# A pre-norm decoder layer on one core: two more block transfers of each duo on GpSimd's queue, other durations in the list, one feed-forward for the last two tiles, and the first rows loaded together

## Chip, core and metric

The kernel runs on one core of a Trainium2 chip. The metric is the device time of one execution in microseconds (us). The kernel before was run three times: 1815.37 us median (1815.3 to 1822.67). The profile is of one further execution.

Engines: TensorE (PE; PEld is its weight load), VectorE (DVE), ScalarE (ACT), GpSimd (POOL), SyncE (SP, which here only issues DMAs; SPq is its queue). DMAs are issued by SP, ACT or POOL, and their bytes are moved by 16 DMA engines.

## What is computed

The input `x` has 4 batches of 1024 rows of 256 numbers in float32. Three sublayers follow one another, each on a normalized copy of `x`:

```
x = x + self_attention(layernorm(x))      # 16 heads of 64, 4 key/value heads
x = x + cross_attention(layernorm(x))     # 16 heads of 16, 64 context rows
x = x + feed_forward(layernorm(x))
```

Self-attention is a full softmax over 1024 keys, with no mask. Cross-attention has a mask over the context rows. The feed-forward routes each row: scores against 8 cluster signatures pass through a calibration curve (a sigmoid and a table of 8 knots), the best cluster is taken, the same is done for the 8 entries of that cluster, and the chosen one of 64 table rows gives a small spline and a direction. The direction, scaled by the spline's value, is added to the normalized row, and the sum is normalized again.

## The kernel before, in words

**Tiles.** A tile is 128 rows of `x`; there are 8 per batch (NT), 32 in all. For one tile there are eight chunks of two heads (QC), and a *duo* (`duo`, from L608) handles two chunks, four heads: 128 duos in all.

**A duo.** TensorE computes scores (L631) for two chunks into PSUM; VectorE takes the largest of each row of 1024 (L645); ScalarE takes the exponential (L651) into `prob`; VectorE transposes `prob` in 32x32 blocks (L660). Sixteen DMAs of 128 KB each (L683 to L695, recorded at L689) then carry the blocks to their places in `probT`, so that together a full transpose results. TensorE multiplies `probT` by the values (L712, `av`), and ScalarE copies the result to `heads` (L727). `prob` and `probT` take slots of one pool of five buffers of 16 KB per partition, tag `prob`.

Of a duo's sixteen block transfers, fourteen are issued by SyncE and two by GpSimd (those with `k == 3` and odd `qb`). All sixteen wait for the four transposes of their duo.

**After four duos (`project`).** The softmax denominators are inverted, go to DRAM and come back spread over partitions (`rsD`, `rb`, on SyncE's queue, L758 and L748); GpSimd multiplies `heads` by them (L751); TensorE applies the output weights (L769, `po`); GpSimd adds the result to `x` (L775).

**Cross-attention** runs for two tiles at a time, its wide steps on GpSimd (L900, L909, L923, L924, L931). In the last tile alone (`last`) they are on VectorE.

**Feed-forward** runs for four tiles at a time (TF). The fifth and sixth tile of the last batch have one of two tiles, and the last two tiles have one each. Each has normalizations (`layernorm`: two statistics instructions on VectorE at L444 and L445, four small steps on GpSimd at L449 to L452, one on ScalarE at L457), a transpose (L471, L475), routing (L1153, L1164), two calibrations and selections (L1005 to L1067, L1183, L1184), an indirect DMA from GpSimd per tile that gathers the chosen rows of the table (L1201), the spline (L1221 to L1236), a second normalization, three last steps (L1253) on GpSimd, and the store (L1263). For the very last tile (`last`), the three last steps are on VectorE, the store on SyncE, and the buffers are cuts of the freed `xT` buffer. The tile before it takes the ordinary ones, with its normalized rows in the `kT1` buffer.

**The order of the work** is made before the kernel runs, by a list scheduler (`Flow`). Each task is added with an engine, a planned duration, a key, what it reads and writes, and a lag between its end and the start of who reads it. At each step the scheduler takes the task that could start earliest by the planned durations; ties go to urgent tasks, then to the smaller key. A task marked `hurry` goes ahead of another that would only be done after the urgent one could start. So the planned durations execute nothing, but they set the order of instructions on every engine, and each engine and DMA queue then works in that order.

A buffer is taken by the first task that names it. Every other task that uses the same buffer then needs that first task's end, and its lag, where it is over 1, also on the same engine:

```python
            elif b.first is not t:
                t.need.add(b.first)
...
                o.ready = max(o.ready, t.end + (t.lag if o.engine != t.engine or t.lag > 1 else 0.0))
```

**The first rows.** `normed` loads a batch's rows in four DMAs of two tiles each (L518). For the first batch the four are cuts of one buffer of tag `prob`, with keys -80 to -77 and lags of 3.5 to 6.5. The weights and masks that SyncE loads have keys -40 to -31.

Of the kernel before, what the change touches and what calls it, by code (L numbers as in the profile page):

```python
# [9 lines left out]
F32 = mybir.dt.float32  # L10
# [6 lines left out]
P = 128  # L17
B, S, D = 4, 1024, 256
NT = S // P
TX, TF = 2, 4  # L20
DC = D // P
H, KV, HD = 16, 4, 64
QC = H * HD // P
# [4 lines left out]
NTILES, NCL, TPC, GRID, COMP, NK = 64, 8, 8, 16, 64, 8  # L28
# [182 lines left out]
def decoder(  # L211
# [221 lines left out]
    def layernorm(key, name, src, dst, w, reads, writes):  # L433

        st = Buf("ln", lambda k: (
            small.tile([P, w, 6], F32, tag=f"bnst_{k}", name=f"{name}_st", bufs=1),
            small.tile([P, w, 2], F32, tag=f"bnmv_{k}", name=f"{name}_mv", bufs=1),
            small.tile([P, w], F32, tag=f"bnrs_{k}", name=f"{name}_rs", bufs=1),
        ))

        def stats():
            bn, mv, _ = st.t
            for t in range(w):
                nc.vector.bn_stats(bn[:, t, :], src(t))  # L444
                nc.vector.bn_aggr(mv[:, t, :], bn[:, t, :])  # L445

        def rsqrt():
            _, mv, rs = st.t
            nc.gpsimd.tensor_scalar(rs, mv[:, :, 1], EPS, None, ALU.add)  # L449
            nc.gpsimd.tensor_tensor(rs, rs, minus_half.to_broadcast([P, w]), ALU.pow)  # L450
            nc.gpsimd.tensor_tensor(mv[:, :, 1], mv[:, :, 0], rs, ALU.mult)
            nc.gpsimd.tensor_scalar(mv[:, :, 1], mv[:, :, 1], -1.0, None, ALU.mult)  # L452

        def apply():
            _, mv, rs = st.t
            for t in range(w):
                nc.scalar.activation(dst(t), src(t), AF.Identity, bias=mv[:, t, 1:2], scale=rs[:, t : t + 1])  # L457

        add("DVE", 0.58 * w, key, stats, reads, [st], holds=writes)
        add("POOL", 1.3, key, rsqrt, [st], [st])  # L460
        add("ACT", 0.57 * w, key, apply, [st, *reads], writes)

    def transposed(key, name, src, dst, k, reads, write, w=2):
# [41 lines left out]
    def normed(b, key):  # L505

        xTs[b] = buf("xT", big, DC, S, name=f"ln1_{b}_T")
        parts = x[b].rearrange("(g t p) d -> g p t d", p=P, t=2)

        whole = None if b else Buf("prob", lambda k: work.tile([P, 4 * S], F32, tag=f"prob_{k}", name="ln1_first", bufs=1))  # L510
        for g in range(NT // 2):
            if b:
                n = buf("xn1", big, 2, D, name=f"ln1_{b}_{g}_n")
            else:
                n = Cut(whole, lambda t, g=g: t[:, 2 * D * g : 2 * D * (g + 1)].rearrange("p (t d) -> p t d", t=2))
            at = key(g)
            add(
                "SP", 0.5, at - 2 if b else -80 + g, lambda n=n, g=g: nc.sync.dma_start(out=n.t, in_=parts[g]), writes=[n],  # L518
                lag=3.5 if b else 3.5 + g,
            )  # L520
            get = lambda t, n=n: n.t[:, t, :]
            layernorm(at, f"ln1_{b}_{g}", get, get, 2, [n], [n])
            transposed(at, f"ln1_{b}_{g}", get, lambda: xTs[b].t, g, [n], xTs[b].part(g))
# [81 lines left out]
    def duo(b, d):  # L605
# [73 lines left out]
        if not by_array(b, d):  # L679


            for k in range(4):
                for qb in range(4):  # L683
                    r = (qb + k) % 4

                    engine, queue, cost = ("POOL", nc.gpsimd, 1.0) if k == 3 and qb % 2 else ("SP", nc.sync, 0.64)

                    def carry(qb=qb, r=r, queue=queue):
                        queue.dma_start(  # L689
                            out=probT.t[32 * r : 32 * r + 32, S * qb : S * (qb + 1)],  # L690
                            in_=prob.t[32 * qb : 32 * qb + 32, S * r : S * (r + 1)],
                        )

                    add(
                        engine, cost, at, carry, [prob.part((z, i)) for z in range(2) for i in range(2)],  # L695
                        [probT.part((z, g)) for z in range(2) for g in range(2)], lag=2.3,
                    )
# [291 lines left out]
            add("POOL", 0.73, now + 4, residual, [r, xp], [xp])  # L989


    def calibrated(at, name, score, w, reads, scratch=None):

        n = w * NCL

        def new(k, tag, *shape):
            return small.tile([P, *shape], F32, tag=f"{tag}_{k}", name=f"{name}_{tag}", bufs=1)

        c = scratch or Buf("cal", lambda k: (
            new(k, "cf", n), new(k, "chot", NK - 1, n), new(k, "clow", n), new(k, "cpick", NK - 1, n), new(k, "cval0", n), new(k, "cval1", n),  # L1000
        ))
        no3 = step_no.unsqueeze(2)
# [67 lines left out]
        add("DVE", 0.4, at, second, [m], [m])  # L1070
        return m

    def feed_forward(b, t0, w, at, last=False, before=False):
        name = f"{b}_{t0}"
        n = w * P
        xp = [x_part(b, t0 + t) for t in range(w)]
# [4 lines left out]
        def cut(*shape):  # L1081

            k = 1
            for i in shape:
                k *= i
            a = taken[0]
            taken[0] = a + k
            dims = " ".join(f"d{i}" for i in range(len(shape)))
            sizes = {f"d{i}": shape[i] for i in range(1, len(shape))}
            return lambda t: t.rearrange("p c s -> p (c s)")[:, a : a + k].rearrange(f"p ({dims}) -> p {dims}", **sizes)  # L1090

        def one(f):
            return Cut(whole, f)

        def several(*f):
            return Cut(whole, lambda t: tuple(g(t) for g in f))

        xf = one(cut(w, D)) if last else flat_buf(*(("kT1", big, S) if before else ("xf", big, TF * D)), f"ln3_{name}_n", w, D)
        xT = one(cut(DC, n)) if last else flat_buf("fp", big, TF * GT, f"ln3_{name}_T", DC, n)
        for t in range(w):  # L1100
            layernorm(
# [13 lines left out]
        some = cut(n)  # L1115
        hT = one(lambda t: some(t)[:COMP]) if last else flat_buf("xhalf", work, 512, f"hT_{name}", n, rows=COMP)
        ph, pc = psum1(f"pch_{name}"), psum1(f"pcomp_{name}")
        comp = one(cut(w, 2)) if last else Buf("comp", lambda k: small.tile([P, w, 2], F32, tag=f"comp_{k}", name=f"comp_{name}", bufs=1))

        def compress():  # L1120
            for dc in range(DC):
# [22 lines left out]
        flow.hurry = last  # L1144


        sc = one(cut(w, NS)) if last else Buf("sc", lambda k: small.tile([P, w, NS], F32, tag=f"sc_{k}", name=f"sc_{name}", bufs=1))
        pr = psum1(f"pr_{name}")

        def route():  # L1150
# [12 lines left out]
            "DVE", 0.46, at + 2,  # L1163
            lambda: nc.vector.tensor_copy(sc.t.rearrange("p t n -> p (t n)"), pr.t[:, : w * NS]), [pr], [sc],  # L1164
        )
        m = w * NCL
        cal = several(cut(m), cut(NK - 1, m), cut(m), cut(NK - 1, m), cut(m), cut(m)) if last else None
        c, gates = calibrated(at + 4, f"cc_{name}", lambda: sc.t[:, :, :NCL], w, [sc], cal)
        ch = first_max(at + 5, f"cm_{name}", gates, w, [c])
        wide = [P, w, NCL, TPC]  # L1170
        index = Buf("index", lambda k: small.tile([P, w], mybir.dt.int32, tag=f"tile_{k}", name=f"tile_{name}", bufs=1))
        hot = several(cut(w, NCL, TPC), cut(w, TPC), cut(w)) if last else Buf("hot", lambda k: (
            small.tile(wide, F32, tag=f"hot_{k}", name=f"hot_{name}", bufs=1),
            small.tile([P, w, TPC], F32, tag=f"sel_{k}", name=f"sel_{name}", bufs=1),
            small.tile([P, w], F32, tag=f"tno_{k}", name=f"tno_{name}", bufs=1),
# [14 lines left out]
            nc.vector.tensor_scalar(idx, no, float(NCL * TPC + NCL), None, ALU.add)  # L1190

        add("DVE", 0.4 + 0.15 * w, at + 6, select, [sc, ch], [hot])
        c, gates = calibrated(at + 7, f"cl_{name}", lambda: hot.t[1], w, [hot], cal)
        lh = first_max(at + 8, f"lm_{name}", gates, w, [c])
        add("DVE", 0.45, at + 9, chosen, [lh, ch, hot], [hot, index])

# [2 lines left out]
        for t in range(w):  # L1199
# [8 lines left out]
            add("POOL", 1.05, at + 11, gather, [index], [par.part(t)], lag=3.0)  # L1208


        hh = several(cut(w, GRID), cut(w, GRID), cut(w)) if last else Buf("hh", lambda k: (
            small.tile([P, w, GRID], F32, tag=f"hh_{k}", name=f"hh_{name}", bufs=1),
            small.tile([P, w, GRID], F32, tag=f"h2_{k}", name=f"h2_{name}", bufs=1),
            small.tile([P, w], F32, tag=f"mag_{k}", name=f"mag_{name}", bufs=1),
# [54 lines left out]
    for b in range(B):  # L1269
        at = float(b * steps_of)  # L1270
        normed(b, lambda g: at - 18 + 2 * g if b else -50 + g)
        for w in range(NT // 2):
            if w == 0:
                keys(b, 0, at - 5)
            for c in range(0, QC, 2):
                queries(b, w, c, at + 2 * QC * w + c - 5)
            if w == 0:
                keys(b, 1, at - 1)
                for g in range(NT // 2):
                    value_rows(b, g, at + g / 2)  # L1280
                for g in range(NT // TF):
                    load_x(b, g, at + 2 + 4 * g * QC)
                context(b, at + 10)
            for d in range(QC * w, QC * w + QC):
                duo(b, d)
                if d % (QC // 2) == QC // 2 - 1:
                    project(b, d // (QC // 2))
            t = 2 * w + 1
            if b == B - 1 and w == NT // 2 - 1:

                for k in (t - 1, t):
                    flow.hurry = k == t
                    cross_attention(b, k, 1, at + QC * (k + 1) + 3, k == t)
                    feed_forward(b, k, 1, at + QC * (k + 1) + 6, k == t, k != t)
                continue
            cross_attention(b, t - TX + 1, TX, at + QC * (t + 1) + 3)
            last = TX if (b, t // TF) == (B - 1, NT // TF - 1) else TF
            if t % last == last - 1:
                feed_forward(b, t - last + 1, last, at + QC * (t + 1) + (10 if last == TF else 7))
# [93 lines left out]
```

## Time and profile before

| | |
|---|---|
| profiled execution, its own time | 1819.6 us |
| its span, first to last instruction | 1817.7 us |
| mean granted TensorE clock | 0.943 |
| GpSimd: block transfers, issues x mean | 256 x 533 ns = 136 us |
| GpSimd: idle before its block transfers | 256.8 us |
| TensorE busy, 150 to 250 us | 96.5% |
| TensorE busy, 400 to 410 us | 85.5% |
| TensorE busy, 1700 to 1710 us | 0% |
| DMA bytes, mean rate over the span | 310.18 MB, 171 GB/s |
| first scores (L631) | 34.99 us |
| last TensorE instruction for attention (L769) ends | about 1733 us |

How to read the views: times count from the first instruction. A line of the timeline has start, length, engine and line of the program, what is written from what, and in brackets how long the engine was idle before it and what ended that. The chain of waits follows the work that ended last backwards to what released each step. A busy TensorE is not TensorE at its peak, since matmuls are pipelined. The share of the DMA engines in a stretch is worked out from packet times and can come a little above 1.

### The profile page before, as it was taken

How to read it: one execution, taken by the hardware profiler on the slowest of the kernel's cores; microseconds unless marked ns; L12 is line 12 of the kernel's file. 1: busy time of each engine (PE TensorE's matmuls, PEld its weight loads, DVE VectorE, ACT ScalarE, POOL GpSimd, SP SyncE). 2: the span in 40 equal slices, each digit the busy share in tenths (PEclk: the TensorE clock that was granted, in tenths of full speed). 3: DMA queues.
4: the chain of work that ended last, by engine and by line, in shares of the span. 5: the costliest groups of instructions: out<-in, count | busy, mean ns of one | idle time of the engine just before them, and what ended most of it. 6: DMA issues, size and time to landing. Idle time of an engine off the chain costs nothing.

```text
span 1817.7 us, 28586 instructions
## 1 busy us (share of the span) xinstructions
PE 1597.9 (88%) x9168; PEld 905.3 (50%) x9168; DVE 1523.4 (84%) x2094; ACT 964.6 (53%) x1793; POOL 756.1 (42%) x1156
## 2 busy tenths in 40 slices
PE   6899999998999789998999889998999979998551
PEld 4354555554555445554555445554555534554331
DVE  4889998889878989888888899889896988889365
ACT  3455565656455456655465456565464544564231
POOL 1112435337251554437243464428333264343643
PEclk9899999999999999999999999999999988999665
DMA  4779888757786588866877578876877478785500
GB/s 143 172 181 222 192 205 211 198 140 179 186 198 151 119 209 211 192 170 168 199 185 171 140 180 204 194 188 171 205 186 173 105 183 201 188 203 151 125 8 19
DMA packets 120148, 310.18 MB, mean 171 GB/s; under 512 B 36576, under 2 KB 47712, under 8 KB 120000
## 3 DMA queue, kind: packets, MB, share of 16 engines
q1 hardware_dynamic: 103936, 263.09, 59.8%
q0 software_dynamic: 14960, 42.90, 9.1%
q10 hardware_dynamic: 1104, 2.37, 0.3%
q8 instruction: 74, 1.21, 0.3%
q14 instruction: 74, 0.61, 0.1%
HBM read 35.32 MB, written 4.46 MB: 22 GB/s over the span
## 4 chain that ended last, share of the span: by engine, by line
PE 47%; DVE 18%; SPq 9%; DMA 8%; POOL 7%; ACT 5%; issue 5%; DVEq 0%; POOLq 0%; ACTq 0%
PE s L631 16%; PE av L712 16%; SPq L689 8%; DVE nmax L645 7%; DMA probT<-prob 5%; DVE prob L660 5%; PE po L769 4%; ACT prob L651 3%; PE pq L584 3%; POOL ln_n L1253 2%; DMA rb<-rsD 1%; PE pxp L978 1%; PE pv L556 1%; PE pk L533 1%; PE pxt L944 1%
## 5 line engine op out<-in xcount | busy, mean ns | idle before, releaser
L651 ACT ACTIVATE prob<-s,nmax 128x1024 f32<-128x1024 f32 x512 | 569.9, 1115 | 356.9 <-DVE nmax L645 318.9
L645 DVE TENSOR_REDUCE nmax<-s 128x1 f32<-128x1024 f32 x512 | 598.5, 1209 | 127.4 <-PE s L631 124.6
L660 DVE STREAM_TRANSPOSE prob<-prob 128x1024 f32<-128x1024 f32 x512 | 612.8, 1223 | 42.1 <-ACT prob L651 19.1
L631 PE MATMUL s<-kT,qT 64*128 64x512 f32 x2048 | 566.3, 628 | 31.2 <-ACT prob L651 25.2
L712 PE MATMUL av<-probT,vn 128*64 128x256 f32 x4096 | 507.8, 398 | 45.1 <-DMA probT<-prob 16.9
L712 PEld LDWEIGHTS av<-probT,vn 128*64 128x64 f32 x4096 | 293.3, 142 | 275.2 <-issue 99.1
L631 PEld LDWEIGHTS s<-kT,qT 64*128 64x128 f32 x2048 | 204.9, 189 | 258.4 <-issue 175.0
L689 POOL DMA_DIRECT2D probT<-prob x256 | 136.0, 533 | 256.8 <-DMA probT<-prob 96.2
L751 POOL TENSOR_TENSOR heads<-heads,rb 128x256 f32<-128x256 f32 x128 | 91.8, 735 | 158.4 <-ACT heads L727 93.4
L769 PE MATMUL po<-wo,heads 128*128 128x256 f32 x512 | 128.5, 395 | 16.9 <-POOL heads L751 13.8
L584 PE MATMUL pq<-ln_T,wq 128*128 128x256 f32 x512 | 127.5, 396 | 9.4 <-ACT heads L727 4.0
L900 POOL TENSOR_TENSOR xsc<-xsc,mneg 128x1024 f32<-128x1024 f32 x31 | 73.7, 2379 | 122.9 <-ACT xsc L892 122.7
L769 PEld LDWEIGHTS po<-wo,heads 128*128 128x128 f32 x512 | 94.0, 193 | 55.8 <-POOL heads L751 28.1
L584 PEld LDWEIGHTS pq<-ln_T,wq 128*128 128x128 f32 x512 | 96.1, 194 | 42.1 <-issue 14.5
L651 ACT ACTIVATION_READ_ACCUMULATOR prob<-s,nmax 128x1 f32 x512 | 100.5, 196 | 0.0
L727 ACT COPY heads<-av 128x256 f32<-128x256 f32 x128 | 47.0, 367 | 84.0 <-PE av L712 83.6
L449 POOL TENSOR_SCALAR ln_rs<-ln_mv 128x1 f32<-128x1 f32 (+1 forms) x97 | 21.7, 224 | 166.5 <-DVE ln_mv L445 135.5
L595 ACT ACTIVATE qT<-pq,bqs,qscale 128x256 f32<-128x256 f32 x128 | 66.4, 561 | 34.7 <-PE pq L584 34.5
L931 POOL TENSOR_TENSOR xsc<-xsc,xrs 128x1024 f32<-128x1024 f32 x31 | 59.0, 1904 | 35.6 <-DVE xrs L928 31.0
L909 POOL TENSOR_TENSOR xsc<-xsc,xmx 128x1024 f32<-128x1024 f32 x31 | 59.2, 1910 | 32.2 <-DVE xmx L906 32.1
L913 ACT ACTIVATE xsc<-xsc 128x1024 f32<-128x1024 f32 x32 | 33.8, 1056 | 66.0 <-POOL xsc L909 63.5
L944 PE MATMUL pxt<-ident,xsc 128*128 128x128 f32 x256 | 41.6, 297 | 30.4 <-POOL xsc L931 16.8
(222 smaller groups left out, 1461.8 us busy)
## 6 DMA issues: line engine op xcount, KB each, us to landing
probT<-prob SPq DMA_DIRECT2D x1792, 128.0 KB
probT<-prob POOLq DMA_DIRECT2D x256, 128.0 KB, 3.8
rb<-rsD SPq DMA_DIRECT2D x64, 256.0 KB
x<-in_x SPq DMA_DIRECT2D x8, 512.0 KB
out<-ln_n POOLq DMA_DIRECT2D x7, 512.0 KB, 4.5
ln_n<-in_x SPq DMA_DIRECT2D x12, 256.0 KB
ln_first<-in_x SPq DMA_DIRECT2D x4, 256.0 KB
wo<-in_w_oT SPq DMA_DIRECT2D x1, 1024.0 KB
```

Source lines behind the costliest of these rows:

```text
L584: mm(pq.t[:, 2 * P * k : 2 * P * (k + 1)], lhsT=wq[:, dc, (c + k) * P : (c + k + 1) * P], rhs=xTs[b].t[:, dc, 2 * P * w : 2 * P * (w + 1)] ...
L595: nc.scalar.activation(qTs[b, w, c + k].t, pq.t[:, 2 * P * k : 2 * P * (k + 1)], AF.Identity, bias=bqs[:, c + k : c + k + 1], scale=qscale,)
L631: mm(ps[z].t[:, 512 * g : 512 * (g + 1)], lhsT=q.t[r, (qt % 2) * P : (qt % 2 + 1) * P], rhs=kT.t[r, 512 * g : 512 * (g + 1)], start=True, ...
L645: nc.vector.tensor_reduce(nmax.t, ps[z].t, AX.X, ALU.max, negate=True)
L651: nc.scalar.activation(weights(prob.t, z, i), src, AF.Exp, bias=nmax.t, accum_out=ss.t[:, k : k + 1])
L660: nc.vector.transpose(t, t)
L689: queue.dma_start(out=probT.t[32 * r : 32 * r + 32, S * qb : S * (qb + 1)], in_=prob.t[32 * qb : 32 * qb + 32, S * r : S * (r + 1)],)
L712: mm(av.t[r, : 2 * P], lhsT=vns[b, kc // 2].t[:, kc % 2, j * HD : (j + 1) * HD], rhs=rhs, start=(kc == 0), stop=(kc == NT - 1),)
L751: nc.gpsimd.tensor_tensor(hT[e].t, hT[e].t, rb.t[:, 2 * e : 2 * e + 2, :], ALU.mult)
L769: mm(po.t[:, :D], lhsT=hT[c // 2].t[:, c % 2], rhs=wo[:, c, :], start=(c == 0), stop=(c == QC - 1))
L900: wide.tensor_tensor(sc.t, sc.t, mneg[:, b, :].unsqueeze(1).to_broadcast([P, XH, SK]), ALU.add)
L944: flip(pt.t[:, j * P : (j + 1) * P], flat[:, c * P : (c + 1) * P], ident)
```

## The change

It has four parts.

1. Four block transfers of a duo (all with `k == 3`) are issued by GpSimd, twelve by SyncE.
2. Three planned durations in the list differ: 0.55 for 1.0 for a block transfer from GpSimd, 0.6 for 0.64 for one from SyncE, 1.6 for 1.3 for the four GpSimd steps of a normalization.
3. The last two tiles have one feed-forward together, marked `last`, after both cross-attentions. Its rows, transposed rows, `hT` and gathered rows are cuts of the freed `xT`; `comp`, `sc`, `cal`, `hot` and `hh`, cuts before, are ordinary buffers now.
4. A task that does nothing, on SyncE with key -90 and no duration, is the first to name the buffer of the first rows, so that the four loads need that task instead of the first load.

```diff
-        add("POOL", 1.3, key, rsqrt, [st], [st])
+        add("POOL", 1.6, key, rsqrt, [st], [st])
...
+        if whole:
+            add("SP", 0.0, -90, None, holds=[whole])
...
-                    engine, queue, cost = ("POOL", nc.gpsimd, 1.0) if k == 3 and qb % 2 else ("SP", nc.sync, 0.64)
+                    engine, queue, cost = ("POOL", nc.gpsimd, 0.55) if k == 3 else ("SP", nc.sync, 0.6)
...
-    def feed_forward(b, t0, w, at, last=False, before=False):
+    def feed_forward(b, t0, w, at, last=False):
...
-        xf = one(cut(w, D)) if last else flat_buf(*(("kT1", big, S) if before else ("xf", big, TF * D)), f"ln3_{name}_n", w, D)
+        xf = one(cut(w, D)) if last else flat_buf("xf", big, TF * D, f"ln3_{name}_n", w, D)
...
                 for k in (t - 1, t):
                     flow.hurry = k == t
                     cross_attention(b, k, 1, at + QC * (k + 1) + 3, k == t)
-                    feed_forward(b, k, 1, at + QC * (k + 1) + 6, k == t, k != t)
+                feed_forward(b, t - 1, 2, at + QC * (t + 1) + 6, True)
```

More of the change, by code (lines that the diff above doesn't have):

```diff
@@ L989, in cross_attention, with calibrated @@
             add("POOL", 0.73, now + 4, residual, [r, xp], [xp])
-    def calibrated(at, name, score, w, reads, scratch=None):
+    def calibrated(at, name, score, w, reads):
         n = w * NCL
@@ L997, in new @@
             return small.tile([P, *shape], F32, tag=f"{tag}_{k}", name=f"{name}_{tag}", bufs=1)
-        c = scratch or Buf("cal", lambda k: (
+        c = Buf("cal", lambda k: (
             new(k, "cf", n), new(k, "chot", NK - 1, n), new(k, "clow", n), new(k, "cpick", NK - 1, n), new(k, "cval0", n), new(k, "cval1", n),
@@ L1093, in one @@
             return Cut(whole, f)
-        def several(*f):
-            return Cut(whole, lambda t: tuple(g(t) for g in f))
-        xf = one(cut(w, D)) if last else flat_buf(*(("kT1", big, S) if before else ("xf", big, TF * D)), f"ln3_{name}_n", w, D)
+        xf = one(cut(w, D)) if last else flat_buf("xf", big, TF * D, f"ln3_{name}_n", w, D)
         xT = one(cut(DC, n)) if last else flat_buf("fp", big, TF * GT, f"ln3_{name}_T", DC, n)
@@ L1117, in feed_forward @@
         ph, pc = psum1(f"pch_{name}"), psum1(f"pcomp_{name}")
-        comp = one(cut(w, 2)) if last else Buf("comp", lambda k: small.tile([P, w, 2], F32, tag=f"comp_{k}", name=f"comp_{name}", bufs=1))
+        comp = Buf("comp", lambda k: small.tile([P, w, 2], F32, tag=f"comp_{k}", name=f"comp_{name}", bufs=1))
         def compress():
@@ L1144, in feed_forward @@
         flow.hurry = last
-        sc = one(cut(w, NS)) if last else Buf("sc", lambda k: small.tile([P, w, NS], F32, tag=f"sc_{k}", name=f"sc_{name}", bufs=1))
+        sc = Buf("sc", lambda k: small.tile([P, w, NS], F32, tag=f"sc_{k}", name=f"sc_{name}", bufs=1))
         pr = psum1(f"pr_{name}")
@@ L1165, in feed_forward @@
         )
-        m = w * NCL
-        cal = several(cut(m), cut(NK - 1, m), cut(m), cut(NK - 1, m), cut(m), cut(m)) if last else None
-        c, gates = calibrated(at + 4, f"cc_{name}", lambda: sc.t[:, :, :NCL], w, [sc], cal)
+        c, gates = calibrated(at + 4, f"cc_{name}", lambda: sc.t[:, :, :NCL], w, [sc])
         ch = first_max(at + 5, f"cm_{name}", gates, w, [c])
@@ L1171, in feed_forward @@
         index = Buf("index", lambda k: small.tile([P, w], mybir.dt.int32, tag=f"tile_{k}", name=f"tile_{name}", bufs=1))
-        hot = several(cut(w, NCL, TPC), cut(w, TPC), cut(w)) if last else Buf("hot", lambda k: (
+        hot = Buf("hot", lambda k: (
             small.tile(wide, F32, tag=f"hot_{k}", name=f"hot_{name}", bufs=1),
@@ L1192, in feed_forward @@
         add("DVE", 0.4 + 0.15 * w, at + 6, select, [sc, ch], [hot])
-        c, gates = calibrated(at + 7, f"cl_{name}", lambda: hot.t[1], w, [hot], cal)
+        c, gates = calibrated(at + 7, f"cl_{name}", lambda: hot.t[1], w, [hot])
         lh = first_max(at + 8, f"lm_{name}", gates, w, [c])
@@ L1208, in feed_forward @@
             add("POOL", 1.05, at + 11, gather, [index], [par.part(t)], lag=3.0)
-        hh = several(cut(w, GRID), cut(w, GRID), cut(w)) if last else Buf("hh", lambda k: (
+        hh = Buf("hh", lambda k: (
             small.tile([P, w, GRID], F32, tag=f"hh_{k}", name=f"hh_{name}", bufs=1),
```

## The prediction

> **What bounds the kernel now.** I read the page's engine shares and chain first, then SyncE's own timeline, then the block transfers as a tile, then stretches, then both ends. From the page:
>
> ```profile
> PE 1597.9 (88%) x9168; PEld 905.3 (50%) x9168; DVE 1523.4 (84%) x2094; ACT 964.6 (53%) x1793; POOL 756.1 (42%) x1156
> PE 47%; DVE 18%; SPq 9%; DMA 8%; POOL 7%; ACT 5%; issue 5%; DVEq 0%; POOLq 0%; ACTq 0%
> ```
>
> TensorE and VectorE are nearly full, and yet 9% of the chain lies on SyncE's queue; the chain by line puts 8% of the span, 145 us, at L689, the block transfers. SyncE's timeline of the stretch from 100 to 260 us says why:
>
> ```profile
> 154.47 29.89 SPq L689 DMA_DIRECT2D probT<-prob  x41
> 186.57 0.33 SPq L758 DMA_DIRECT2D rsD<-rsT  x1
> 187.08 0.51 SPq L689 DMA_DIRECT2D probT<-prob  x1
> 188.02 1.11 SPq L748 DMA_DIRECT2D rb<-rsD  x2
> 189.19 31.22 SPq L689 DMA_DIRECT2D probT<-prob  x41
> ```
>
> Columns: start, length, queue and line, count. 83 transfers, six duos of 14 less one, take from 154.47 to 220.41: 66 us, 11.1 us a duo, and the queue hardly rests. The tile's answer has the issue times (ns, least/median/most):
>
> ```profile
> L689 SPq DMA_DIRECT2D probT<-prob x1792: 507/590/2196, 48.2 to 1711.1; - x200
> L689 POOL DMA_DIRECT2D probT<-prob x256: 492/518/741, 48.5 to 1717.2; - x128
> DMA to landing us min/median/max: 2.4/3.8/6.1
> ```
>
> The 2196 is an issue held up. By what, and where GpSimd is full instead, the stretches show (columns: length, busy time of PE, PEld, DVE, ACT, POOL; clock, share of the DMA engines, GB/s):
>
> ```profile
> 410.00:420.00 10.00, 8.70 (x42) 4.50 (x40) 9.76 (x15) 7.19 (x15) 8.76 (x20) 1.00 0.12 27
> 420.00:430.00 10.00, 9.28 (x73) 5.25 (x70) 10.00 (x11) 6.36 (x13) 9.19 (x14) 1.00 0.79 185
> 616.00:620.00 4.00, 4.00 (x18) 2.39 (x18) 2.84 (x5) 0.92 (x2) 3.86 (x5) 1.00 1.04 245
> 620.00:624.00 4.00, 2.06 (x8) 0.78 (x7) 3.79 (x10) 2.08 (x4) 1.12 (x3) 1.00 1.03 244
> 1700.00:1710.00 10.00, 0.00 (x0) 0.00 (x0) 2.65 (x6) 1.06 (x1) 9.16 (x11) 0.50 0.87 241
> ```
>
> In a dense burst (616 to 624) the DMA engines are full at 245 GB/s; in a feed-forward's stretch (410 to 430) GpSimd is 90% busy; near the end (1700 to 1710) TensorE does nothing while GpSimd works, and duo 126's two GpSimd transfers leave only at 1705.58 and 1713.97.
>
> **Start: first rows at once, -5 us.** The timeline of the first 45 us:
>
> ```profile
> 0.81 0.44 SPq L518 DMA_DIRECT2D ln_first<-in_x  x1
> 11.11 7.13 PE L584 MATMUL pq<-ln_T,wq 128*128 128x256 f32 x24 [1.96 <-DMA wq<-in_w_qT]
> 14.11 1.69 SPq L518 DMA_DIRECT2D ln_first<-in_x  x3
> 23.78 2.02 PE L471 MATMUL ln_pt<-ident,ln_first 128*128 128x128 f32 x8 [5.54 <-ACT qT L595]
> 34.99 1.99 PE L631 MATMUL s<-kT,qT 64*128 64x512 f32 x8
> ```
>
> The list has loads 2 to 4 wait for load 1 with its lag (3.5), since it took their common buffer; seven weight and mask loads fill that time, two of them (cT) take 7.99 us, and the rows are issued at 14.11. With an empty task taking the buffer at no lag, the four loads are first on SyncE by key. They then issue at some 0.5 us each (0.44 to 0.59 here), by 3 us. At the bursts' 245 GB/s, 1 MB of rows and about as much from ScalarE's queue beside it need 8 us, so the rows are in by 9 instead of 17. Three normalizations (DVE 1.2, POOL 1.6, ACT 1.1, pipelined) end by 13, behind the 24 query matmuls that wait for wq until 11.11. The 5.54 us gap before 23.78 closes: -5.5, and +0.5 for wq, which shares its bandwidth with the rows. What is late next is wq, then VectorE, which the chain follows from 37 to 68 us. The seven displaced loads go 1.7 us later; wo is first read at 98 us. Bounds: -9 (the 1.96 and more of the gaps go too) to +2 (wq 3 us later, nothing else gained).
>
> **Tail: one feed-forward, -8 us.** The timeline from 1766 us on:
>
> ```profile
> 1772.93 1.13 PE L1153 MATMUL pr<-sig,ffn 128*128 128x72 f32 x4 [0.46 <-ACT ffn L475]
> 1781.29 1.13 PE L1153 MATMUL pr<-sig,ln_T 128*128 128x72 f32 x4 [2.06 <-DVE ffn L1140]
> 1796.20 0.42 DVE L1253 TENSOR_TENSOR ffn<-ffn,x 128x256 f32<-128x256 f32 x1
> 1800.94 1.08 POOL L1201 DMA_INDIRECT par<-in_table,tile  x1 [6.32 <-DVE tile L1190]
> 1810.66 0.72 POOL L1253 TENSOR_TENSOR ln_n<-ln_n,x 128x256 f32<-128x256 f32 x1
> ```
>
> The last tile (ffn) is done at 1796.62; the tile before it, routed 8.4 us later and never urgent, at 1811.38. One feed-forward of both starts with the last tile's and pays for width two. Rows of the two-tile feed-forward at 1735 to 1743 against the one-tile rows at 1782 to 1790: eight wider VectorE instructions per calibration differ by 0.05 to 0.09 each, 0.54, twice, 1.1; selection and copy 0.3; flips and their copy 0.7; four more routing matmuls 1.1; a second gather 1.6 (1757.55 to 1759.15); a second move 0.5; the second normalization's four GpSimd steps 1.5. Sum 6.8: the end is 1803.4 instead of 1811.4, -8. The store follows on SyncE (0.37 us issue against 0.68 on GpSimd). Its scratch buffers, now shared with the feed-forward before it, are free: that one selects at 1741 and moves by 1771, the new one needs them from 1774 and 1790. Bounds: -12 (routing at no extra cost, the other tile's instructions no longer in between) to +5 (its cross-attention isn't urgent, and now the urgent feed-forward waits for it).
>
> **Bulk: two more transfers of each duo from GpSimd, new durations, -8 us.** SyncE loses 256 issues: at 0.59 and a gap of 0.04, 1.26 us a duo. If SyncE's whole part in the chain shrank with its count, 145 x 2/14 = -21: the bound of gain. Little of this can stay, for two reasons: TensorE was busy 96.5, 96.9, 97.4 and 96.8% in the stretches 150:250, 250:350, 850:950 and 1550:1650, and in dense bursts the DMA engines, not the issue, set the pace (16 transfers of 128 KB at 245 GB/s need 8.6 us; SyncE's 14 issues at 0.63 need 8.8, its 12 would need 7.6). GpSimd gets 256 x 0.53 = 136 us more, 756 to 892, 49% of the span. That lies beside other work except where GpSimd is full. The instruction waits at GpSimd's head for all four transposes of its duo; behind it stand the normalizations, the head divisions that TensorE's po waits for (13.8 us in the waits) and the cross-attention. The other durations in the list (0.6 for 0.64, 0.55 for 1.0, 1.6 for 1.3) execute nothing; they reorder, and the trace can't say how. The measured 0.63, 0.53 and 1.6 (18.85 to 20.47) speak for them at two places of three. Bounds -21 to +35 (rival 3); I take -8, two fifths of the gain: the DMA engines are at 95% or above in only 5 of the 40 ten-us stretches from 100 to 500, which speaks for more, and TensorE's idle 3% of the steady stretches for less.
>
> A rule to weigh: the Trainium skill, "DMA: Bandwidth & Descriptors", section "Issuing engines are not separate DMA queues", says that DMAs run on the same 16 engines whoever starts them, and that several issuers save only the sequencer's issue time. The rows of 616 to 624 agree; by that rule alone the bulk term would be 0, and the sum 8 us higher.
>
> Another speaks against GpSimd: "SBUF — State Buffer", section "A bandwidth-pool intuition that's wrong (but worth ruling out)", has a GpSimd DMA of 0.62 us grow to 3.1 beside a VectorE copy. The row here, at most 0.741 us to issue, shows nothing of it; 256 transfers at 2.5 us more would be 640 us.
>
> **Sum.** -5 -8 -8 = -21. The profiled execution took 1819.6 us (span 1817.7 and 1.9 around it): 1798.6. It stood 4.2 above the median of the runs shown (1815.4), from which the same sum gives 1794.4. I predict 1797, between the two.
>
> **Rivals.** (1) SyncE was the real bound of the steady stretches: with 1.26 us less per duo, TensorE closes up and the whole bound of 21 us comes, with -5 and -12 at the ends; -38, 1779. For it: SyncE's timeline; against it: TensorE's 97%. (2) The gains don't last: VectorE, which holds the chain from 37 us on, eats the earlier start, the new order gives nothing, and only the tail's 8 us stay: 1809, within 0.5%. The change then does only a third of what it says. (3) GpSimd becomes the bound in the feed-forward stretches. Place: six stretches such as 410:430 and the last at 1690:1717. Price: four duos each, 2 more issues of 0.53 and 0.09 gap, 5 us a stretch, 35 in seven. It decides from about 95% of GpSimd: 1.3 duos in 20 us add 1.6 us, 8%, to 88 and 92%, so it is close. With -5 and -8 at the ends, +22: 1837. For it: duo 126's late transfers, for which TensorE stood; against it: elsewhere GpSimd's pair mostly leaves well before SyncE's last.
>
> **How the numbers follow.** Forecast 0.40 (1797, own range 1785 to 1806), rival 1 0.15, rival 2 0.22, rival 3 0.23. Half a per cent, 9 us, is about what a measurement of this kernel can tell from no change. Faster by more: 0.40 + 0.15 = 0.55; within: 0.22; slower: 0.23. The range takes in rival 1 with some room (-42, all bounds of gain: 1773) and rival 3 up to 1830, which leaves out its larger half and little else.
>
> **What would show it.** Start: four L518 issues before any weight's, first scores near 30 us instead of 34.99. Tail: one routing of eight matmuls, no GpSimd L1253 after VectorE's last. Bulk: 1536 SyncE and 512 GpSimd issues, SPq below 7% in the chain, and POOL not over its 7%. I am wrong if TensorE's idle time grows in stretches where GpSimd is full, if its transfers leave after SyncE's last in many duos, or if VectorE's order makes scores wait.

## The result, and the profile after

The changed kernel is slower: 1880.5 us median (1871.2 to 1885.3) against 1815.3; the ratio is 1.0327, 95% interval 1.0298 to 1.0357. The forecast was 1797. The profiled execution of the changed kernel took 1871.2 us, with a span of 1869.5, 51.8 more than before.

**Both ends gained, more than forecast.** The timeline of the first 45 us, after:

```profile
0.80 2.04 SPq L520 DMA_DIRECT2D ln_first<-in_x  x4
...
10.59 3.62 PE L586 MATMUL pq<-ln_T,wq 128*128 128x256 f32 x8
...
23.97 1.99 PE L633 MATMUL s<-kT,qT 64*128 64x512 f32 x8
```

The four loads go first, wq is no later, and the first scores start at 23.97 instead of 34.99. The end of the timeline:

```profile
1836.71 1.99 PE L1152 MATMUL pr<-sig,ffn 128*128 128x72 f32 x8 [0.68 <-ACT ffn L475]
...
1853.70 0.95 POOL L1198 DMA_INDIRECT ffn<-in_table,tile  x1 [0.30 <-issue]
...
1864.64 0.42 DVE L1250 TENSOR_TENSOR ffn<-ffn,x 128x256 f32<-128x256 f32 x1
1865.09 0.40 SPq L1260 DMA_DIRECT2D out<-ffn  x1
```

There is one routing of eight matmuls and one chain behind it. Cut where the values (`av`) of the first and of the last duo start, the difference of 51.8 us is -10.5 before the first cut (62.7 to 52.2), +74.9 between the two (1662.6 to 1737.5; this stretch is called the bulk below) and -12.6 behind the second (92.4 to 79.8).

**All of the loss lies in between.** The page after:

```profile
PE 1613.6 (86%) x9164; PEld 910.5 (49%) x9164; DVE 1522.8 (81%) x2047; ACT 959.6 (51%) x1788; POOL 874.5 (47%) x1408
...
PE 39%; DVE 17%; SPq 15%; DMA 13%; POOL 6%; issue 4%; ACT 4%; DVEq 0%; POOLq 0%; ACTq 0%
PE av L714 14%; SPq L691 14%; PE s L633 13%; DMA probT<-prob 9%; DVE nmax L647 5%; DVE prob L662 4%; PE po L771 2%; ACT prob L653 2%; POOL ln_n L1250 2%; PE pq L586 2%; DMA par<-in_table,tile 2%; PE pxq L858 1%; POOL par L1198 1%; PE pxp L980 1%; PE pv L558 1%
```

SyncE issues a seventh fewer block transfers, and yet its part in the chain rose from 9 to 15%, and the DMAs' from 8 to 13%; GpSimd's fell. What TensorE waited for between 40 and 1760 us, in us, times and longest, first before, then after:

```profile
PE av L712 <- DMA probT<-prob: 16.9, 8, 3.7
```

```profile
PE av L714 <- DMA probT<-prob: 79.0, 18, 12.5
```

62 us more of waiting for transfers to land, in few long waits. The stretches say where (columns as in the prediction). First three of before, then five of after:

```profile
350.00:450.00 100.00, 93.15 (x502) 50.45 (x498) 88.56 (x140) 58.28 (x107) 52.55 (x80) 0.95 0.65 163
650.00:750.00 100.00, 95.50 (x570) 51.72 (x567) 90.75 (x102) 58.91 (x111) 45.99 (x67) 0.97 0.83 203
1050.00:1150.00 100.00, 91.16 (x552) 49.58 (x550) 91.48 (x108) 58.87 (x111) 54.00 (x87) 0.97 0.79 195
```

```profile
350.00:450.00 100.00, 79.15 (x442) 44.57 (x440) 78.98 (x123) 48.90 (x91) 54.65 (x81) 0.95 0.58 143
650.00:750.00 100.00, 83.50 (x480) 44.99 (x478) 80.53 (x91) 52.04 (x98) 56.65 (x91) 0.90 0.78 196
1050.00:1150.00 100.00, 78.56 (x422) 43.73 (x424) 80.72 (x126) 44.75 (x85) 58.14 (x90) 0.86 0.60 150
950.00:1050.00 100.00, 96.97 (x596) 57.15 (x594) 83.11 (x96) 58.69 (x110) 44.72 (x67) 1.00 0.72 179
1350.00:1450.00 100.00, 96.91 (x557) 55.86 (x557) 80.50 (x86) 52.29 (x98) 43.80 (x67) 0.97 0.75 180
```

The last two still have TensorE at 97%; the first three, each with the last steps of a feed-forward in it, fall to 79 to 84%. (The same time is not quite the same work in the two kernels.) Four waits of 8 to 12 us for a transfer, ended at 440.8, 670.8, 1120.5 and 1561.9 us, come 11 to 14 us behind a feed-forward's last steps. The first of them, GpSimd's timeline and then TensorE's:

```profile
427.23 0.89 POOL L1260 DMA_DIRECT2D out<-ln_n  x1 [0.30 <-POOL ln_n L1250]
428.14 2.37 POOL L902 TENSOR_TENSOR xsc<-xsc,mneg 128x1024 f32<-128x1024 f32 x1
430.45 0.73 POOL L986 TENSOR_TENSOR x<-x,xres 128x256 f32<-128x256 f32 x1
431.12 1.03 POOL L691 DMA_DIRECT2D probT<-prob  x2
432.17 1.91 POOL L911 TENSOR_TENSOR xsc<-xsc,xmx 128x1024 f32<-128x1024 f32 x1
434.02 0.51 POOL L691 DMA_DIRECT2D probT<-prob  x1
435.42 0.51 POOL L691 DMA_DIRECT2D probT<-prob  x1 [0.89 <-issue]
```

```profile
430.46 1.99 PE L633 MATMUL s<-kT,qT 64*128 64x512 f32 x8
440.79 5.88 PE L714 MATMUL av<-probT,vn 128*64 128x256 f32 x32 [8.34 <-DMA probT<-prob]
```

Duo 30's transfers from SyncE are out by 421; GpSimd's follow a feed-forward's last steps and end at 435.9. This looks like rival 3. The transfers as a tile, after:

```profile
L691 SPq DMA_DIRECT2D probT<-prob x1536: 507/591/2304, 36.8 to 1780.6; - x192
L691 POOL DMA_DIRECT2D probT<-prob x512: 489/492/762, 37.1 to 1781.5; - x171
DMA to landing us min/median/max: 2.1/4.2/8.1
```

and SyncE's own timeline between 100 and 200 us:

```profile
125.32 26.61 SPq L691 DMA_DIRECT2D probT<-prob  x32
...
174.78 22.67 SPq L691 DMA_DIRECT2D probT<-prob  x29
```

The median issue still takes 0.59 us, but these took 0.83 and 0.78 each. From a duo's first SyncE issue to the end of its last passed 9.86 us before (median of the 128 duos, from the trace) and 9.56 after: twelve take nearly as long as fourteen did.

### The profile page after: what moved, and what is told of

The parts are those of the page before. It is cut to its first block, busy times and chain, and to the rows that moved or that the text cites. A ratio compares the mean times of both kernels' runs of the same rounds, so it can differ in the third digit from the quotient of the medians.

```text
span 1869.5 us, 29099 instructions
## 1 busy us (share of the span) xinstructions
PE 1613.6 (86%) x9164; PEld 910.5 (49%) x9164; DVE 1522.8 (81%) x2047; ACT 959.6 (51%) x1788; POOL 874.5 (47%) x1408
## 4 chain that ended last, share of the span: by engine, by line
PE 39%; DVE 17%; SPq 15%; DMA 13%; POOL 6%; issue 4%; ACT 4%; DVEq 0%; POOLq 0%; ACTq 0%
PE av L714 14%; SPq L691 14%; PE s L633 13%; DMA probT<-prob 9%; DVE nmax L647 5%; DVE prob L662 4%; PE po L771 2%; ACT prob L653 2%; POOL ln_n L1250 2%; PE pq L586 2%; DMA par<-in_table,tile 2%; PE pxq L858 1%; POOL par L1198 1%; PE pxp L980 1%; PE pv L558 1%
## 5 line engine op out<-in xcount | busy, mean ns | idle before, releaser
L714 PE MATMUL av<-probT,vn 128*64 128x256 f32 x4096 | 515.9, 401 | 117.2 <-DMA probT<-prob 80.3
L633 PE MATMUL s<-kT,qT 64*128 64x512 f32 x2048 | 576.3, 628 | 27.5 <-ACT prob L653 27.3
L714 PEld LDWEIGHTS av<-probT,vn 128*64 128x64 f32 x4096 | 299.5, 143 | 346.8 <-issue 172.4
L691 POOL DMA_DIRECT2D probT<-prob x512 | 259.2, 512 | 297.5 <-DVE prob L662 135.9
L771 PEld LDWEIGHTS po<-wo,heads 128*128 128x128 f32 x512 | 99.1, 200 | 53.0 <-POOL heads L753 25.7
L986 POOL TENSOR_TENSOR x<-x,xres 128x256 f32<-128x256 f32 x32 | 23.3, 729 | 102.1 <-DVE xres L983 102.1
```

The costliest lines, as they stand in the source:

```text
L633: mm(ps[z].t[:, 512 * g : 512 * (g + 1)], lhsT=q.t[r, (qt % 2) * P : (qt % 2 + 1) * P], rhs=kT.t[r, 512 * g : 512 * (g + 1)], start=True, ...
L691: queue.dma_start(out=probT.t[32 * r : 32 * r + 32, S * qb : S * (qb + 1)], in_=prob.t[32 * qb : 32 * qb + 32, S * r : S * (r + 1)],)
L714: mm(av.t[r, : 2 * P], lhsT=vns[b, kc // 2].t[:, kc % 2, j * HD : (j + 1) * HD], rhs=rhs, start=(kc == 0), stop=(kc == NT - 1),)
L771: mm(po.t[:, :D], lhsT=hT[c // 2].t[:, c % 2], rhs=wo[:, c, :], start=(c == 0), stop=(c == QC - 1))
```

## Theories

*Theory 1* (rival 3): GpSimd's queue, fuller and in order, makes transfers late. *Theory 2*: the three new durations make an order that counts on transfers faster than they are. *Theory 3* came after the first four runs: the list counts on less time for a duo's transfers than the DMA engines need.

The list's own time for a duo's SyncE transfers follows from the scheduler: the first takes the buffer, the others wait for its end and its lag of 2.3, then come one by one, so it is 2.3 + count x duration: 11.3 us before (14 x 0.64), 9.5 after (12 x 0.6). The *list's end*, below, is the time at which the last task of the list ends by the planned durations: 1776 us before, 1773 after.

## Experiments

Before ran beside each group: 1825.2, 1822.9 and 1825.0 us median. Ratios are to it.

**1. Only the queue** (before, its own list):

```diff
+                    queue = nc.gpsimd if k == 3 else nc.sync
```

> The kernel before with its own list and order; only the two transfers with k == 3 and even qb leave from GpSimd's queue instead of SyncE's, at the same places of the order. If GpSimd's queue and load make the loss (theory 1, rival 3 of the prediction), most of it appears here: 1850 to 1870 us. If the list's new durations make it, by an order that counts on transfers faster than they are (theory 2), this stays within 10 us of the kernel before.

1889.3 us, 1.035 (1.032 to 1.038). The loss is there, as theory 1 expected, and is larger than its 1850 to 1870. But the two moved transfers now stand among GpSimd's instructions where the list had meant SyncE's: in 81 of 128 duos GpSimd's last issue ends after SyncE's last (before 12, after 18). So it shows what a badly placed GpSimd transfer costs, more than what the change did.

**2. Only the list** (the changed kernel, its own list):

```diff
+                    queue = nc.gpsimd if k == 3 and qb % 2 else nc.sync
```

> The changed kernel with its own list; only the two transfers with k == 3 and even qb leave from SyncE's queue again, at the same places of the order. Theory 1: 1800 to 1815 us, since the start and the tail are gained and GpSimd is relieved. Theory 2: 1860 to 1890, the order is the same.

1875.9 us, 1.029 (1.025 to 1.033). Giving two transfers back to SyncE recovers nothing that the intervals separate: theory 1 alone can't stand. Most of the loss comes with the order.

**3. The new durations alone** (before):

```diff
-        add("POOL", 1.3, key, rsqrt, [st], [st])
+        add("POOL", 1.6, key, rsqrt, [st], [st])
...
-                    engine, queue, cost = ("POOL", nc.gpsimd, 1.0) if k == 3 and qb % 2 else ("SP", nc.sync, 0.64)
+                    engine, queue, cost = ("POOL", nc.gpsimd, 0.55) if k == 3 and qb % 2 else ("SP", nc.sync, 0.6)
```

> The kernel before with the three new durations alone (0.55, 0.6, 1.6), two transfers from GpSimd. Theory 1: within 15 us of before. Theory 2: slower by 30 to 60.

1833.4 us, 1.004 (1.002 to 1.006). Theory 2 falls as stated: the three durations alone, with fourteen transfers on SyncE, cost 0.4%.

**4. Four transfers at the old durations** (before):

```diff
-                    engine, queue, cost = ("POOL", nc.gpsimd, 1.0) if k == 3 and qb % 2 else ("SP", nc.sync, 0.64)
+                    engine, queue, cost = ("POOL", nc.gpsimd, 1.0) if k == 3 else ("SP", nc.sync, 0.64)
```

> The kernel before with four transfers from GpSimd at the old durations (1.0, 0.64, 1.3). Theory 1: 1850 to 1880 us, GpSimd as loaded as in the changed kernel. Theory 2: near before, 1810 to 1830, since GpSimd's transfers are priced high enough to be late in the list as well.

1894.5 us, 1.038 (1.034 to 1.041), above the 1850 to 1880 of theory 1 and far from theory 2. The count matters, at either set of durations. Theories 1 and 3 are left: with count 12 the list gives a duo 10.0 us here, where fourteen had 11.3.

**8. GpSimd's transfers first** (changed kernel):

```diff
-                        [probT.part((z, g)) for z in range(2) for g in range(2)], lag=2.3,
+                        [probT.part((z, g)) for z in range(2) for g in range(2)], lag=2.3, urgent=engine == "POOL",
```

> The changed kernel with GpSimd's four transfers marked urgent, so that of the work ready on GpSimd they go first. Its list ends at 1757 us, the changed kernel's at 1773, the one of before at 1776. Theory 1 (the transfers stand too far behind in GpSimd's queue): 1800 to 1825 us. Theory 3 (the list reckons a duo's twelve SyncE issues no longer than they are, so that time lost in a feed-forward's stretch is never made up): the list's end and nearly the same 95 us on it, about 1850.

1858.1 us, 1.020 (1.015 to 1.025). Now GpSimd's last issue is behind SyncE's in 1 duo of 128, and the kernel still ends 101 us after its list. It is some 22 us faster than the changed kernel, its list ends 16 us earlier, and its bulk is 42.8 us longer than before instead of 74.9, so late GpSimd transfers may be a part of the loss. That is against theory 1 as the whole cause, which had 1800 to 1825; for theory 3, which had about 1850.

**9. Less work for GpSimd** (changed kernel, same list; gamma and beta are left out of all feed-forwards but the last):

```diff
+                if not last and k < 2:
+                    return
```

> The changed kernel, same list, without the gamma and beta steps of the feed-forwards other than the last (the computation leaves these out): eight GpSimd steps of 0.75 us less in each of six feed-forwards of four tiles, and four in one of two, 39 us of GpSimd in all, none on other engines. If the loss begins where GpSimd is full, 30 to 40 us come back: 1840 to 1850. If it lies in the steady stretches: within 10 us of the changed kernel.

1870.3 us, 1.028 (1.022 to 1.035). By the pages of the two profiles 60 steps are gone, 43 us of GpSimd's work (the expectation counted 39), from its fullest places; some 10 us come back, which the intervals don't tell from nothing. How much GpSimd has to do isn't what decides.

**10. One number of the list** (changed kernel):

```diff
-                    engine, queue, cost = ("POOL", nc.gpsimd, 0.55) if k == 3 else ("SP", nc.sync, 0.6)
+                    engine, queue, cost = ("POOL", nc.gpsimd, 0.55) if k == 3 else ("SP", nc.sync, 0.74)
```

> The changed kernel with a SyncE transfer planned at 0.74 instead of 0.6, so that the list gives a duo's twelve the 11.2 us that it gave fourteen before. Its list ends at 1798 us. Theory 3: the list then overestimates as before, and the time on top of the list's end falls from 100 to about 45 us: 1835 to 1850. Theory 1: the time on top stays near 90: 1885 to 1900.

1826.8 us, 1.002 (0.999 to 1.005). Four transfers from GpSimd as in the changed kernel, and the time is that of before. Theory 1 had 1885 to 1900; theory 3 had 1835 to 1850, and the run is faster than that. Not all of the loss is gone: in the profiled executions the bulk takes 22.4 us more than before, instead of 74.9, and the gains at both ends make up for it. The transfers as a tile, here:

```profile
L691 SPq DMA_DIRECT2D probT<-prob x1536: 507/591/2478, 36.6 to 1725.2; - x192
L691 POOL DMA_DIRECT2D probT<-prob x512: 489/492/762, 36.9 to 1727.2; - x171
```

Counts and the median issue times are as in the changed kernel; a duo's twelve take 9.48 us, nearly as there (9.56). The transfers are no faster; the order allows for them.

**7. Start and tail without the transfers** (two from GpSimd, durations of before):

```diff
-        add("POOL", 1.6, key, rsqrt, [st], [st])
+        add("POOL", 1.3, key, rsqrt, [st], [st])
...
-                    engine, queue, cost = ("POOL", nc.gpsimd, 0.55) if k == 3 else ("SP", nc.sync, 0.6)
+                    engine, queue, cost = ("POOL", nc.gpsimd, 1.0) if k == 3 and qb % 2 else ("SP", nc.sync, 0.64)
```

> The changed kernel's first rows and its one feed-forward for the last two tiles, with two transfers from GpSimd and the durations of before. All theories: the start's 11 us and the tail's 13, seen between the traces of before and after, stay: 1790 to 1805 us, 1 to 1.5 per cent faster than before.

1799.7 us, 0.988 (0.983 to 0.993): faster than both kernels, and as expected. First scores at 25.50. Cut as above, its profiled execution has -9.0 us before the first duo's values, +1.2 in the bulk and -14.5 behind the last. So run 10, which has both ends as well, gains nothing by its two moved transfers: it is 27 us slower than this one.

**11 and 12. Half of the bytes** (before, and the changed kernel):

```diff
-                            out=probT.t[32 * r : 32 * r + 32, S * qb : S * (qb + 1)],
-                            in_=prob.t[32 * qb : 32 * qb + 32, S * r : S * (r + 1)],
+                            out=probT.t[32 * r : 32 * r + 32, S * qb : S * qb + S // 2],
+                            in_=prob.t[32 * qb : 32 * qb + 32, S * r : S * r + S // 2],
...
-                            rhs = probT.t.rearrange("p (b z i c q) -> p b z i c q", b=4, z=2, i=2, q=32)[:, :, z, :, kc]
+                            rhs = probT.t.rearrange("p (b z i c q) -> p b z i c q", b=4, z=2, i=2, q=32)[:, :, 0, :, kc]
```

> The kernel before, each block transfer carrying half of its columns (64 KB instead of 128), TensorE's values reading the carried half twice; the other half of each pair of heads is left out of the result. Same list, same instructions otherwise. It is the partner of the next run: 1785 to 1815 us.

> The changed kernel with the same halving (and the same part left out). If the DMA engines hold SyncE's twelve issues up to the time of fourteen, and the list has no slack for that (theory 3), the twelve now take 7.6 us against the 9.5 in the list, and the kernel ends near its list: 1785 to 1810 us. If GpSimd's queue makes the loss (theory 1), which does not depend on the bytes, 1850 to 1875.

Before with half: 1787.2 us, 0.981 (0.976 to 0.986). The changed kernel with half: 1778.9, 0.977 (0.972 to 0.983), 6 us past its list's end (theory 3 had 1785 to 1810, theory 1 1850 to 1875), and now the faster of the two; that comes from its ends, its bulk is still 9 us longer than run 11's. It has the instructions and the list of the slow kernel; the bytes differ. Dense stretches of the changed kernel (last two columns: share of the DMA engines, GB/s):

```profile
100.00:104.00 4.00, 4.00 (x27) 1.89 (x26) 3.24 (x4) 0.66 (x1) 0.00 (x0) 1.00 0.92 248
175.00:179.00 4.00, 4.00 (x15) 2.29 (x16) 3.86 (x4) 3.44 (x5) 2.33 (x3) 1.00 1.02 285
252.00:256.00 4.00, 4.00 (x29) 2.20 (x27) 3.86 (x5) 2.60 (x5) 0.58 (x3) 1.00 0.93 243
```

and the same stretches with half of the bytes, with its tile:

```profile
100.00:104.00 4.00, 4.00 (x26) 2.60 (x24) 3.73 (x4) 3.12 (x7) 1.99 (x4) 1.00 0.44 115
175.00:179.00 4.00, 4.00 (x32) 2.25 (x31) 3.58 (x4) 2.39 (x5) 0.65 (x2) 1.00 0.59 163
252.00:256.00 4.00, 4.00 (x25) 2.50 (x24) 3.86 (x4) 2.33 (x4) 2.65 (x5) 1.00 0.52 138
```

```profile
L691 SPq DMA_DIRECT2D probT<-prob x1536: 507/589/2201, 35.7 to 1682.6; - x192
L691 POOL DMA_DIRECT2D probT<-prob x512: 498/498/763, 36.0 to 1685.2; - x171
```

With the engines half idle, a duo's twelve take 7.76 us instead of 9.56, near 12 x 0.63. So what holds the issues up is how busy the DMA engines are. Half of the bytes also land sooner (GpSimd's in 2.4 us, median, instead of 4.2), so this run doesn't tell a late issue from a late landing; run 10 changes neither.

**13. The same fault without the change** (before, two transfers from GpSimd):

```diff
-                    engine, queue, cost = ("POOL", nc.gpsimd, 1.0) if k == 3 and qb % 2 else ("SP", nc.sync, 0.64)
+                    engine, queue, cost = ("POOL", nc.gpsimd, 1.0) if k == 3 and qb % 2 else ("SP", nc.sync, 0.515)
```

> The kernel before, two transfers from GpSimd as it was, with a SyncE transfer planned at 0.515 instead of 0.64, so that the list gives a duo's fourteen 9.5 us, as the changed kernel's gives its twelve, and the chip needs 9.9. Its list ends at 1809 us. Theory 3: some 85 us on top, 1880 to 1900, though nothing is moved to GpSimd. Theory 1: 40 us on top as in the kernel before, 1840 to 1855.

1871.8 us, 1.028 (1.023 to 1.033). Nothing is moved, and the time is nearly that of the changed kernel. Its bulk is 45.3 us longer than before, against 74.9. It is 63 us past its list's end: more than theory 1's 40, less than the 85 expected of theory 3. Its chain has SyncE at 16%, where the changed kernel has 15:

```profile
PE 35%; DVE 17%; SPq 16%; DMA 11%; POOL 8%; ACT 7%; issue 5%; DVEq 0%; POOLq 0%; ACTq 0%
```

**14. A size between** (changed kernel):

```diff
-                    engine, queue, cost = ("POOL", nc.gpsimd, 0.55) if k == 3 else ("SP", nc.sync, 0.6)
+                    engine, queue, cost = ("POOL", nc.gpsimd, 0.55) if k == 3 else ("SP", nc.sync, 0.67)
```

> The changed kernel with a SyncE transfer planned at 0.67 (10.3 us a duo in the list, 9.5 on the chip). Its list ends at 1797 us, as that of the run with 0.74. Theory 3 says the time on top lies between those of 0.6 (100) and 0.74 (29): 1835 to 1860.

1863.1 us, 1.023 (1.018 to 1.029), just past the upper end of what was expected; 66 us past the list's end, between the 107 of 0.6 and the 29 of 0.74. It is 17 us faster than the changed kernel (its five executions took 1860.2 to 1877.5), and 0.74 brings 36 more.

**All together.** The SyncE time of a duo in the list and on the chip (median), the list's end, the measured median and the difference of the two, in us:

| kernel | list | chip | list's end | measured | past it |
|---|---|---|---|---|---|
| changed kernel | 9.5 | 9.6 | 1773 | 1880.5 | 107 |
| 2, only the list | 9.5 | 9.8 | 1773 | 1875.9 | 103 |
| 8, urgent | 9.5 | 9.6 | 1757 | 1858.1 | 101 |
| 9, less work | 9.5 | 9.5 | 1773 | 1870.3 | 97 |
| 13, cheap | 9.5 | 9.6 | 1809 | 1871.8 | 63 |
| 4, four at old durations | 10.0 | 9.5 | 1813 | 1894.5 | 82 |
| 14, 0.67 | 10.3 | 9.4 | 1797 | 1863.1 | 66 |
| 3, durations | 10.7 | 9.8 | 1797 | 1833.4 | 37 |
| 10, 0.74 | 11.2 | 9.5 | 1798 | 1826.8 | 29 |
| before | 11.3 | 9.9 | 1776 | 1815.3 | 39 |
| 7, start and tail | 11.3 | 9.7 | 1762 | 1799.7 | 38 |
| 11, half, before | 11.3 | 9.4 | 1776 | 1787.2 | 11 |
| 12, half, changed | 9.5 | 7.8 | 1773 | 1778.9 | 6 |
| 1, only the queue | 11.3 | 8.8 | 1776 | 1889.3 | 113 |

Where the list allows over 1 us more than the chip needs, the kernel, run 1 apart, ends 6 to 49 us past its list (49 with before at 1825); with less to spare, up to 107. The spare time doesn't settle it alone: runs 3 and 14 both have 0.9, and end 37 and 66 past. With full bytes the list's own column orders them better: 29 to 39 us past at 11.2 and 11.3, 37 at 10.7, 66 at 10.3, 82 at 10.0, 97 to 107 at 9.5. Two runs fall out: run 1, with late GpSimd transfers, and run 13, with 63 at 9.5. This order was seen afterwards; no run was made to test it.

How far behind their planned start the values of a duo start shows where the time goes, in us (minus is ahead of it):

| duo | 8 | 24 | 28 | 32 | 44 | 48 | 64 | 96 | 127 |
|---|---|---|---|---|---|---|---|---|---|
| before | 10.7 | 3.6 | 8.4 | 9.5 | 13.1 | 14.3 | 16.4 | 19.6 | 31.7 |
| changed kernel | 7.3 | 6.4 | 6.0 | 16.7 | 19.1 | 27.6 | 48.0 | 68.1 | 89.6 |
| 10, 0.74 | -5.6 | -12.9 | -6.4 | -6.5 | 0.2 | 1.3 | 4.4 | -0.5 | 12.3 |
| 12, half, changed | -4.4 | -13.6 | -14.0 | -6.7 | -9.3 | -6.2 | -5.6 | -8.3 | -9.6 |

From duo 8 to 24, a steady stretch, before makes up 7.1 us, run 10 7.3, run 12 9.2, the changed kernel 0.9. From 28 to 32, with a feed-forward, the changed kernel falls 10.7 behind, before 1.1, run 10 none, run 12 7.3; but run 12 then holds its place to the end, and the changed kernel falls behind by 73 us more. So the runs whose list leaves time to spare make up time in a steady stretch, and the changed kernel doesn't.

## Why the prediction was wrong, step by step

- **Start**, -5 forecast: right mechanism, mis-sized; the first duo's values came 10.5 us earlier, past the bound of -9. wq was not later, and the order of the start changed too: eight key matmuls (L533, now L535), not sixteen, now stand before the first scores.
- **Tail**, -8 forecast: right mechanism, sized too small; 12.6 behind the last duo's values, just past the bound of -12. From the routing to the last step 10.1 us went, since the second tile cost 4.7 us and not 6.8, and 1.9 behind that step. Run 7, with both ends, gained 1.2%, 22 us, in all.
- **Bulk**, -8 forecast, +74.9 measured: this step failed, at two places; its sign was wrong, not only its size. First, "SyncE loses 256 issues: at 0.59 and a gap of 0.04, 1.26 us a duo": measured 0.3 (9.86 to 9.56). The prediction named the reason, full DMA engines, and used it only to shrink a gain. Second, "The other durations in the list ... execute nothing; they reorder, and the trace can't say how", and that 0.63, 0.53 and 1.6 "speak for them". A warning was there: 12 x 0.6 + 2.3 is 9.5, 16 transfers of 128 KB at 245 GB/s need 8.6, and fourteen took 9.9 with 11.3 in the list. The change took 1.8 us a duo out of the list, where the chip gave back 0.3. The prediction put this term at nothing, and the runs price it: with 0.74 for 0.6 the bulk is 22.4 us longer than before instead of 74.9 (run 10), and 0.515 alone, nothing moved, makes it 45.3 longer (run 13). The bound of +35 came from GpSimd alone and was too low.
- **Rule weighed.** What the Trainium skill says in "DMA: Bandwidth & Descriptors", section "Issuing engines are not separate DMA queues", agrees with these runs: with full bytes moving two issues hardly shortens a duo (9.86 and 9.56), with half of them the issue sets the pace (7.76). It priced the bulk at 0, nearer than my -8 to the measured +74.9; neither had a term for the order.
- **Rival 3** had the sign and the places, TensorE standing in feed-forward stretches; its cause, a full GpSimd, did not hold as the main one: runs 2 and 9 relieve GpSimd, run 8 puts its transfers first, and all stay slow; run 10 does neither and takes the time of before. **Rivals 1 and 2** did not occur. "SPq below 7%" failed most plainly, at 15; GpSimd's transfers left after SyncE's last in 18 duos of 128, against 12 before, which is not many.
- **Left open.** How a tight order turns into time, by full `prob` slots or by what stands ahead on each engine, was not separated, nor why run 13 lost less than the changed kernel at equal list time, nor what makes run 10's bulk 22.4 us longer than before. TensorE's wait for transfers is not the loss by itself: run 12 has 42.2 us of it and ends 6 us past its list. The list also counts 2.3 us from a transfer's end to its landing, where GpSimd's transfers took 3.8 before and 4.2 after (medians, from their issue); no run changed that number. Start and tail were not run apart.

## What to carry to other kernels

A list of planned durations is part of the kernel's speed: before counting a moved instruction as saved, work out how long the group takes when the shared resource behind it (here 16 DMA engines, 243 to 285 GB/s in the full stretches shown) is full, and keep that, with some spare, in the plan. An issue's median time (0.59) is not its price; what a whole group takes from first to last is. Compare an order's planned times with the trace: a lag that grows from stretch to stretch, as the changed kernel's did, is a reason to try a longer duration in the plan; here that one number brought back 52 of 75 us.

## What was not expected of the hardware

SyncE's issues themselves stretch when the DMA engines are full: the mean was 641 ns with fourteen a duo, 719 with twelve and four from GpSimd beside them, 610 with half of the bytes; the median stayed at 589 to 591. With the changed list and two from GpSimd (run 2) the mean was 643. So transfers moved to a second issuer slowed the first.
